# Two-layer graph network: four leaky activations, a maximum and a propagator moved to the far side of the copies of zT

## The chip, the cores and the metric

The kernel runs on one core of a Trainium2 chip. The metric is the device time of one execution in microseconds. Before the change the median of three runs is 2470.5 us (2469.41 to 2471.38). The profiled execution spans 2467.1 us.

The engines are named as in the profile: PE (matrix products; PEld is its loading of weights), DVE (vector), ACT (scalar, activations and copies out of PSUM), POOL (GpSimd) and SP, which only issues DMAs here. Each engine works through its own list of instructions in order. An instruction that waits for another engine holds up everything behind it on its own engine.

## The reference

The input is 128 graphs of 128 nodes with 512 features, `x`, and 128 adjacency matrices of zeros and ones, `adj`. Two layers follow each other, each with a residual and a layer norm:

```python
# layer 0: graph attention, 8 heads of 64
feats = einsum('bnf,hfu->bhnu', x, W)
dense = e_self[..., :, None] + e_neigh[..., None, :]
dense = leaky_relu(dense, 0.2) + NEG_BIG * (1 - A)
att = softmax(dense, axis=-1)
x = layernorm(x + relu(einsum('bhij,bhju->bhiu', att, feats) + b))

# layer 1: two hypergraph convolutions, 512 -> 1024 -> 512
def hypergraph_conv(x, adj, W, b):      # H = (adj != 0)
    xw = einsum('ncd,hd->nch', x, W)
    m = Be * einsum('nce,nch->neh', H, xw)
    return Dn * einsum('nce,neh->nch', H, m) + b
h = layer_norm(relu(hypergraph_conv(x, adj, W1, b1)), gamma, beta)
x = layernorm(x + hypergraph_conv(h, adj, W2, b2) + x)
```

`Dn` and `Be` are reciprocal degrees of nodes and hyperedges. The kernel folds the two products with `H` and both degrees into one 128x128 matrix for each graph, the propagator `R`.

## The kernel before

The graphs are taken in 64 pairs. The work on one pair is cut into some hundred steps, small functions such as `propagate` or `leaky`. Each step has a lag in whole periods and a due time within a period of `T = 38.6`; the step of pair `p` is due at `(p + lag) * T + time`. All steps of all pairs are sorted by due time, and every engine gets its instructions in that order. The due times are only an order: nothing is timed by them. A dictionary `first` gives some steps of the first pairs a due time of their own. A tile framework adds the semaphore waits: an instruction waits for the data it reads, and an instruction that writes a tile waits until the readers of the tile that had the same memory before are done. Tiles come from pools; `work` has one buffer a tag unless `bufs` says otherwise, and PSUM is a ring of eight banks under the tag `bank`.

In the steady state four stages of different pairs lie beside each other in one period. The part around the change, for the pair that is in its second layer ("this pair") and the one a period behind ("the next pair"):

- `first_output` (L780, ACT): writes the normalised result of layer 0 into `y`, for both graphs of this pair.
- `propagate` (L802, PE): `y` times `R`, eight instructions a graph in the trace, into the banks `pz`. `z_evict` (L813, ACT) copies each bank to `zT`. `z_sums` (L822, POOL) makes four sums `zS` from it.
- `hidden` in `chain("ph", 3, ...)` (L833, L846, PE): seven products with the first hidden weights. They use a Strassen-like scheme with seven instead of eight block products. Four of the seven go into the same bank, `phX`. Their order is product 1 (into phX), 2 (phY), 6 (phX), 5 (phW) and 7 (phX), then the two products `pq` of an older pair, then 4 (phX) and 3 (phW). Between two uses of `phX` ACT copies the bank out (`copy`, L329, with `nc.scalar.copy` at L332) and PE then adds the next product on top.
- `masked`, `leaky`, `largest`, `exponential` (L576 to L609): attention of the next pair, for each graph `g` and half of the heads `q`. POOL adds the mask, ACT applies the leaky activation in four instructions (L595), DVE takes the maximum (L601), ACT takes four exponentials (L609). All work in place in the tile `nb`. Then SP writes the result out and reads it back in blocks (L613, L621), and DVE transposes it (L630).
- `propagator` and `r_evict` (L427, L437): two 128x128 products `pd` from `hB` and `hT` (PE, four instructions), and DVE's scaling of it to `R`. `R` is first read one period later. It has three buffers.
- `edges` (L400, DVE): for the pair after the next one. It transposes blocks of the adjacency into `hT` (L409), counts (L411), and makes reciprocal degrees `deg` (L415, L416). `hT` has one buffer, so the write of `hT` for one pair comes after the propagator's reading of `hT` for the pair before.
- `sum_rest` (L960, DVE): sums of squares for the norm of `h`, which came back through DRAM (`so`, `veh`). POOL turns them into `rsh` (L986), DVE scales `y2` by it (L994), and `output` (L1004, PE, `pq`) reads the scaled `y2`.

Before the change the order on PE is: the last `py` products of this pair's predecessor with `pd` between them, then `pz`, then the first `phX`. On ACT it is: `first_output`, eight leaky activations (graph 0), a copy to `y2` (L922), the two copies to `zT`, four leaky activations, the first copy of `phX`, eight exponentials, four leaky activations, the second copy of `phX`, eight exponentials, the third copy. On DVE: `hT`, `deg`, `R`, two maxima, a sum of `y2` (L924), `so` and `veh`, a maximum, a sum of `h` (L855), the scaling of `y2`, a maximum.

Of the kernel before, what the change touches and what calls it, by code (L numbers as in the profile page):

```python
# [20 lines left out]
def kernel(  # L21
# [67 lines left out]
    def bank(name):  # L89
        return psum.tile([P, HALF], F32, tag="bank", name=name)  # L90
# [210 lines left out]
    LAST = PAIRS - 1  # L301
    steps = []

    def step(lag, time, since=0, until=PAIRS):

        def keep(fn):
            steps.append((lag, time, fn.__name__, range(since, until), fn, ()))
            return fn
        return keep

    def at(lag, time, fn, *args, since=0, until=PAIRS):
        steps.append((lag, time, fn.__name__, range(since, until), fn, args))
# [111 lines left out]
                s["hB"][:, g, :], s["hT"][:, g, :], s["be"][:, g:g + 1], None, op0=ALU.mult  # L424
            )

    @step(1, 34.7)  # L427
    def propagator(p, s):

        s["pd"] = bank(f"pd_{p}")  # L430
        for g in range(2):
            nc.tensor.matmul(
                s["pd"][:, g * N:(g + 1) * N], s["hB"][:, g, :], s["hT"][:, g, :],
                start=True, stop=True,
            )

    @step(1, 35.8)  # L437
    def r_evict(p, s):
        s["R"] = work.tile([P, 2, N], F32, tag="R", name=f"R_{p}", bufs=3)
        nc.vector.tensor_tensor(  # L440
            s["R"].rearrange("p g (b n) -> p g b n", b=NB),
            s["pd"][:, :2 * N].rearrange("p (g b n) -> p g b n", g=2, b=NB),
            s["dnb"].rearrange("p b g n -> p g b n"), op=ALU.mult,
        )
# [199 lines left out]
        )  # L644

    for (g, q), tm, (lag, tl), (lagx, tx), te, tt in (
        ((0, 0), 31.0, (1, 33.2), (1, 36.1), 4.05, 16.6), ((0, 1), 32.2, (1, 35.0), (1, 36.7), 4.6, 16.65),
        ((1, 0), 34.2, (2, 2.05), (2, 2.1), 7.8, 21.5), ((1, 1), 35.4, (2, 6.0), (2, 7.3), 7.9, 21.55),
    ):
        at(1, tm, masked, g, q)  # L650
        at(lag, tl, leaky, g, q)
        at(lagx, tx, largest, g, q)
        at(2, te, exponential, g, q)
        at(2, tt, e_transpose, g, q, since=1)
# [254 lines left out]
    def weigh(s, i, to, start):  # L909
# [3 lines left out]
          QU, 1, until=LAST)  # L913
# [43 lines left out]
                s["sd"][:, 2 * c:2 * c + 2, :].rearrange("b g n -> b (g n)"),  # L957
            )

    @step(4, 1.0, until=LAST - 1)  # L960
    def sum_rest(p, s):
        t = work.tile([P, B], F32, tag="so", name=f"so_{p}")
        nc.vector.transpose(t, sums_out)
        s["ve"] = small.tile([P, 2], F32, tag="ve", name=f"veh_{p}")
        nc.vector.tensor_reduce(
            s["ve"], t[:, :2 * NB].rearrange("p (b g) -> p g b", g=2), AX.X, ALU.add
        )
# [147 lines left out]
    for t, fn, *args in (  # L1115
# [44 lines left out]
        ("spread_rows", 1): 15.72, ("nodes", 1): 15.55, ("write_nodes", 1): 15.85,  # L1160
        ("edges", 1): 110.4, ("scale_edges", 1): 110.5, ("neighbours", 1): 80.1,
        ("propagator", 1): 117.76, ("spread_nodes", 1): 80.3, ("r_evict", 1): 121.8,
        ("leaky", 0, 1, 1): 77.65,
        ("attend", 0, 0, 0): 78.95, ("attend", 0, 0, 1): 78.96, ("attend", 0): 97.85,
        ("attended", 0, 0): 99.7, ("attended", 0, 1): 99.8,
        ("leaky", 1, 0, 0): 117.85, ("leaky", 1, 0, 1): 117.9, ("leaky", 1, 1, 0): 119.9,
        ("largest", 1, 0, 0): 118.0, ("largest", 1, 0, 1): 118.2, ("largest", 1, 1, 0): 120.2,
        ("masked", 1, 0, 0): 109.0, ("masked", 1, 1, 1): 121.5,
        ("nodes", 2): 141.0, ("write_nodes", 2): 143.0, ("nodes", 3): 150.0,
        ("write_nodes", 3): 150.1, ("skip", 0): 132.5,  # L1170
    }

# [88 lines left out]
```

## Time and profile before

| | PE | PEld | DVE | ACT | POOL |
|---|---|---|---|---|---|
| busy, us of 2467.1 | 2411.5 | 2148.6 | 1997.5 | 1529.3 | 1797.7 |
| share of the span | 98% | 87% | 81% | 62% | 73% |
| instructions | 18273 | 18273 | 4456 | 4481 | 2060 |

The granted PE clock is 9 tenths or more in each of the 40 slices of the page, and the DMA engines are busy for 0.4 to 0.6 of each but the last two. PE's busy time counts a matmul from its start to its modelled end, and neighbouring matmuls overlap, so a busy PE isn't a PE at its peak. What can be read is where PE is idle: an idle time stands in square brackets after an instruction, with what ended it. A timeline line is: start, length, engine, line, operation, output<-inputs, shapes, how many instructions were merged.

Some costs from the groups of the page and of the trace: a product of `pd`, `pz` or `ph` has a mean of 275 to 281 ns from start to modelled end; a leaky activation 391 ns, an exponential 392 ns, a copy of `phX` 580 ns, all from start to end, with starts closer together than that when they follow each other; a maximum 682 ns; the scaling to `R` 409 ns.

### The profile page before, as it was taken

The page shows a single profiled execution, that of the slowest core. Times are in us where ns is not written, and L with a number is a line of the kernel's source. Part 1 is how long each engine was busy: PE and PEld are TensorE (multiplying, and loading weights), DVE is VectorE, ACT ScalarE, POOL GpSimd, SP SyncE. Part 2 cuts the span into 40 slices and gives each one's busy share as a digit, 9 for nine tenths or more (in the row PEclk, how much of TensorE's full clock was granted, in tenths as well). Part 3 has the DMA queues.
Part 4 walks back from the last instruction along what each step waited for, and adds up shares of the span by engine and source line. Part 5 has one row for each costly group of instructions (what it writes and reads, how often), then busy time and mean ns, then how long its engine had stood idle before and what let it go on. Part 6 is the DMA issues. An engine that isn't in the chain of part 4 may idle for free.

```text
span 2467.1 us, 52770 instructions
## 1 busy us (share of the span) xinstructions
PE 2411.5 (98%) x18273; PEld 2148.6 (87%) x18273; DVE 1997.5 (81%) x4456; ACT 1529.3 (62%) x4481; POOL 1797.7 (73%) x2060
## 2 busy tenths in 40 slices
PE   7999999999999999999999999999999999999998
PEld 5888888888888888888888888888888888888887
DVE  7888788888878887888788888878887888788876
ACT  4565665755756656657566566576575665665763
POOL 5777777777777777767777777777677767777774
PEclk9999999999999999999999999999999999999999
DMA  6545445545445455454455555554544545545531
GB/s 183 137 145 144 145 130 148 146 129 151 141 137 146 143 145 145 128 153 138 134 145 145 142 142 141 148 145 129 151 138 136 147 139 146 143 135 153 142 112 52
DMA packets 432762, 345.30 MB, mean 140 GB/s; under 512 B 153176, under 2 KB 382064, under 8 KB 432496
## 3 DMA queue, kind: packets, MB, share of 16 engines
q1 hardware_dynamic: 429024, 337.46, 48.3%
q10 hardware_dynamic: 3472, 4.47, 0.5%
q8 instruction: 145, 2.38, 0.4%
q14 instruction: 121, 0.99, 0.1%
HBM read 239.08 MB, written 102.73 MB: 139 GB/s over the span
## 4 chain that ended last, share of the span: by engine, by line
PE 55%; DVE 14%; ACT 11%; DMA 11%; POOL 5%; issue 4%; SPq 2%; DVEq 0%; POOLq 0%; ACTq 0%
PE phX L840 17%; PE phW L840 8%; PE pfX L476 8%; ACT nb L595 6%; PE pyX L476 4%; PE phY L840 4%; PE pfW L476 4%; DMA sd<-sr 4%; PE pq L1006 4%; DMA nb<-rd 3%; DVE y L725 3%; ACT y L782 2%; DVE xT L373 2%; DVE y L739 2%; PE pfY L476 2%
## 5 line engine op out<-in xcount | busy, mean ns | idle before, releaser
L332 ACT COPY py<-pyX 128x257 f32<-128x257 f32 x189 | 70.9, 375 | 531.1 <-PE pyX L476 526.6
L840 PEld LDWEIGHTS phX<-zS,w_sb 128*128 128x128 f32 x3072 | 363.1, 192 | 33.0 <-issue 31.6
L840 PE MATMUL phX<-zS,w_sb 128*128 128x128 f32 x3072 | 374.3, 275 | 2.4 <-POOL xS L458 1.3
L893 POOL TENSOR_TENSOR sq<-sq 128x512 f32<-128x512 f32 (+2 forms) x384 | 324.0, 844 | 20.4 <-ACT sq L881 0.3
L579 POOL TENSOR_TENSOR nb<-nb,neg 128x512 f32<-128x512 f32 x256 | 318.5, 1277 | 9.2 <-DMA nb<-rd 9.2
L595 ACT ACTIVATE nb<-nb,ft 128x128 f32<-128x128 f32 x1020 | 317.9, 391 | 7.9 <-POOL nb L579 7.9
L755 POOL TENSOR_TENSOR rso<-veo,mhalf 128x2 f32<-128x2 f32 x63 | 44.2, 701 | 371.6 <-DVE veo L753 371.6
L609 ACT ACTIVATE nb<-nb,nm 128x128 f32<-128x128 f32 x1024 | 313.6, 392 | 0.6 <-DVE nm L601 0.6
L870 ACT ACTIVATE h<-h,vecs 128x128 f32<-128x128 f32 x768 | 244.9, 392 | 42.3 <-DVE h L855 42.3
L476 PE MATMUL pyX<-w_sb,hS 128*128 128x257 f32 x1008 | 245.6, 385 | 0.0
L476 PE MATMUL pyW<-w_sb,hS 128*128 128x256 f32 x1008 | 238.7, 379 | 3.1 <-DVE y L924 2.9
L476 PE MATMUL pyX<-w_sb,h 128*128 128x257 f32 x1008 | 239.5, 379 | 0.5 <-ACT py L332 0.5
L601 DVE TENSOR_REDUCE nm<-nb 128x4 f32<-128x512 f32 x256 | 174.5, 682 | 73.0 <-ACT nb L595 60.7
L476 PEld LDWEIGHTS pyW<-w_sb,hS 128*128 128x128 f32 x1008 | 190.5, 189 | 31.4 <-POOL rsa L755 3.2
L476 PEld LDWEIGHTS pyX<-w_sb,hS 128*128 128x128 f32 x1008 | 185.8, 189 | 28.7
L476 PEld LDWEIGHTS pyX<-w_sb,h 128*128 128x128 f32 x1008 | 186.5, 190 | 25.5 <-ACT py L332 0.9
L499 DVE TENSOR_TENSOR ft<-pf,pfW 128x264 f32<-128x264 f32 x124 | 53.2, 429 | 165.8 <-PE pfW L476 90.1
L630 DVE STREAM_TRANSPOSE eT<-eb 128x512 f32<-128x512 f32 x252 | 163.5, 687 | 0.0
L881 ACT ACTIVATE sq<-h 128x512 f32<-128x512 f32 x256 | 160.4, 627 | 2.1
L730 POOL TENSOR_TENSOR y<-y,b_bc 128x512 f32<-128x512 f32 x128 | 160.3, 1273 | 1.8 <-DVE rden L724 1.5
L458 POOL TENSOR_TENSOR hS<-h 128x512 f32<-128x512 f32 x126 | 158.9, 1281 | 2.3 <-ACT h L870 2.3
L840 PE MATMUL phX<-zT,w_sb 128*128 128x128 f32 x1024 | 131.1, 281 | 26.1 <-ACT zT L817 26.1
(178 smaller groups left out, 5783.5 us busy)
## 6 DMA issues: line engine op xcount, KB each, us to landing
nb<-rd SPq DMA_DIRECT2D x127, 512.0 KB
ed<-nb SPq DMA_DIRECT2D x126, 512.0 KB
eb<-ed SPq DMA_DIRECT2D x504, 128.0 KB
x<-in_x_dram SPq DMA_DIRECT2D x64, 512.0 KB
out_dram<-o SPq DMA_DIRECT2D x63, 512.0 KB
xb<-in_x_dram SPq DMA_DIRECT2D x248, 128.0 KB
a<-in_adj_dram SPq DMA_DIRECT2D x64, 128.0 KB
w<-in_adj_dram SPq DMA_DIRECT2D x128, 64.0 KB
```

Source lines behind the costliest of these rows:

```text
L458: engine.tensor_tensor(t[:, i], in0, in1, op=op)
L476: nc.tensor.matmul(to[:, :n], lhs[:, k, :], rhs[:, k, :n], start=bool(start) and k == 0, stop=(k == nk - 1), skip_group_check=True,)
L579: nc.gpsimd.tensor_tensor(t, t, neg[:, :, None, :].to_broadcast([P, NB, HH, B]), op=ALU.add)
L595: nc.scalar.activation(t, t, AF.Prelu, bias=s["ft"][:, g, h, 0:1], alpha=SLOPE)
L601: nc.vector.tensor_reduce(s["nm"][:, g, hs], scores(p, s, g, hs).rearrange("p b h j -> p h b j"), AX.XY, ALU.max, negate=True,)
L609: nc.scalar.activation(t, t, AF.Exp, bias=s["nm"][:, g, h:h + 1])
L630: nc.vector.transpose(s["eT"][:, g, hs, :].rearrange("p h (b i) -> p h b i", b=NB), s["eb", g][:, :, hs, :].rearrange("p b h j -> p h b j"),)
L730: nc.gpsimd.tensor_tensor(s["y"][:, g, :], s["y"][:, g, :], b0_bc, op=ALU.add)
L840: nc.tensor.matmul(to[:, m * N:(m + 1) * N], w[:, k, m * P:(m + 1) * P], rhs[:, k, :], start=bool(start) and m == 0 and k == 0, stop=(k == ...
L870: nc.scalar.activation(dst[:, k, :], src[:, k, :], AF.Relu, bias=b1_sb[:, c:c + 1])
L881: nc.scalar.activation(s["sq"][:, g, q * KH // 2:(q + 1) * KH // 2, :], hid(s, g, q), AF.Square, scale=DH ** -0.5,)
L893: nc.gpsimd.tensor_tensor(t[:, :n, :], t[:, :n, :], t[:, n:2 * n, :], op=ALU.add)
```

## The change

Three moves, all by due times alone; no instruction is added or removed.

1. On ACT and DVE, the leaky activations of graph 0, second half of the heads (four instructions), and their maximum move behind the two copies of `zT`, to lag 1 at 40.63 and 40.68, which is 2.03 and 2.08 into the period of the propagation.
2. On PE, the next pair's propagator moves from between the last `py` products to between `propagate` and the first hidden product (40.1 is 1.5 into that period). DVE's `r_evict` follows it, and `sum_rest` goes behind that.
3. In the prologue, pair 1 has no step of the first kind to move around, so the old due times of its second half are kept (73.6 and 75.3), and `nodes` of pair 2 is due a step later.

The aim is that ACT comes to the copies of `zT` sooner, and that PE has the propagator's products to do while the copy is made.

```diff
-    @step(1, 34.7)
+    @step(1, 40.1)
     def propagator(p, s):
...
-    @step(1, 35.8)
+    @step(1, 40.2)
     def r_evict(p, s):
...
     for (g, q), tm, (lag, tl), (lagx, tx), te, tt in (
-        ((0, 0), 31.0, (1, 33.2), (1, 36.1), 4.05, 16.6), ((0, 1), 32.2, (1, 35.0), (1, 36.7), 4.6, 16.65),
+        ((0, 0), 31.0, (1, 33.2), (1, 36.1), 4.05, 16.6), ((0, 1), 32.2, (1, 40.63), (1, 40.68), 4.6, 16.65),
         ((1, 0), 34.2, (2, 2.05), (2, 2.1), 7.8, 21.5), ((1, 1), 35.4, (2, 6.0), (2, 7.3), 7.9, 21.55),
...
-    @step(4, 1.0, until=LAST - 1)
+    @step(4, 1.7, until=LAST - 1)
     def sum_rest(p, s):
...
-        ("leaky", 0, 1, 1): 77.65,
+        ("leaky", 0, 1, 1): 77.65, ("leaky", 0, 0, 1): 73.6, ("largest", 0, 0, 1): 75.3,
...
-        ("nodes", 2): 141.0, ("write_nodes", 2): 143.0, ("nodes", 3): 150.0,
+        ("nodes", 2): 142.2, ("write_nodes", 2): 143.0, ("nodes", 3): 150.0,
```

## The prediction

> **What bounds the kernel now.** I read the page's busy shares first: PE is busy for 2411.5 us of 2467.1 (98%), so time can come only from PE's few gaps. Second, the busy sums over two windows, each one pair long (the start of one propagation to the start of the next): both last 37.7 us, PE is idle for 0.4 of it, and no other engine passes 31 us. Third, the table of waits says what that 0.4 us is.
>
> ```profile
> 1037.46:1075.17 37.71, 37.28 (x285) 33.33 (x284) 30.90 (x70) 23.84 (x71) 27.91 (x33) 1.00 0.50 143
> 1075.17:1112.90 37.73, 37.33 (x286) 33.37 (x285) 30.92 (x71) 23.86 (x72) 27.93 (x33) 1.00 0.48 142
> ```
> (Columns: length, busy us of PE, PEld, DVE, ACT, POOL, clock, DMA share, GB/s.)
>
> ```profile
> PEld phX L840 <- ACT zT L817: 37.7, 61, 0.9
> PE phX L840 <- ACT zT L817: 26.1, 61, 0.7
> ```
> 61 times, once a pair, the first hidden product waits for ACT's copy of zT. Last, the timeline around one such wait; all instants below are of this window:
>
> ```profile
> 1071.27 0.61 PE L432 MATMUL pd<-hT,hB 128*128 128x128 f32 x4
> 1071.71 1.90 PE L476 MATMUL pyX<-w_sb,h 128*128 128x256 f32 x8
> ...
> 1072.44 4.98 POOL L579 TENSOR_TENSOR nb<-nb,neg 128x512 f32<-128x512 f32 x4
> ...
> 1072.89 1.50 ACT L782 ACTIVATE y<-y,sh,rsa 128x512 f32<-128x512 f32 x2
> 1072.92 0.44 DVE L409 STREAM_TRANSPOSE hT<-ab 128x256 f32<-128x256 f32 x1
> ...
> 1073.93 1.04 DVE L415 TENSOR_SCALAR deg<-deg 128x2 f32<-128x2 f32 x1
> 1074.30 2.43 ACT L595 ACTIVATE nb<-nb,ft 128x128 f32<-128x128 f32 x8
> ...
> 1075.17 1.95 PE L805 MATMUL pz<-R,y 128*128 128x128 f32 x16
> ...
> 1076.89 1.06 ACT L817 COPY zT<-pz 128x512 f32<-128x512 f32 x2
> ...
> 1077.52 2.05 PE L840 MATMUL phX<-zT,w_sb 128*128 128x128 f32 x16 [0.40 <-ACT zT L817]
> ...
> 1079.41 1.95 PE L840 MATMUL phY<-zT,w_sb 128*128 128x128 f32 x16
> ...
> 1079.61 0.59 ACT L332 COPY ph<-phX 128x512 f32<-128x512 f32 x1 [0.48 <-PE phX L840]
> 1080.09 2.45 ACT L609 ACTIVATE nb<-nb,nm 128x128 f32<-128x128 f32 x8
> ...
> 1083.61 0.56 ACT L332 COPY ph<-phX 128x512 f32<-128x512 f32 x1
> ...
> 1084.77 1.95 PE L840 MATMUL phX<-zS,w_sb 128*128 128x128 f32 x16
> ```
> ACT runs eight leaky activations (0.293 us apart) and a copy before the copies of zT; PE has finished the propagation long before. The real price is more than 0.40: with no wait, 16 matmuls follow in 1.79 us (phY 1079.41 to the next product 1081.20), so from pz at 1075.17 phY would start at 1078.74. It starts at 1079.41: **0.67 us a pair**, made of 0.16 of drain, 0.40 of idle and 0.11 at the first matmul after the wait.
>
> **What the Trainium skill says.** "GPSIMD Engine Reference", Specifications: GpSimd's SBUF interfaces are shared with VectorE, with contention for DVE instructions in a 2-port mode or with two SBUF inputs. "Advanced Engine Details and Errata", Instruction Support: tensor_scalar has such a mode, tensor_reduce none. The trace agrees: deg, a tensor_scalar on 128x2, takes 169 ns at least and 1056 ns in the median; above, it ends at 1074.97, just after the second of POOL's four masks of 1.28 us; the reductions L601 keep to 682 ns beside the same masks. "DVE: scalar operands, raw-bit mode, write accounting and state across instructions", Flops that outlive an instruction, calls the DVE's queue one in-order queue; in this trace the DVE never overtakes a waiting instruction.
>
> **The change, part by part.**
>
> *Propagator behind the propagation (PE).* Nothing is added: 4 matmuls of 0.111 us apiece, 0.44 us, leave their place at 1071.27 and come after pz. So pz starts at 1074.73. Its input is ready: the two activations L782 start 0.70 us apart and take 0.80, so y is there at 1073.69 and 1074.39. pd runs from 1076.51, and the first hidden product can follow at 1076.95, phY at 1078.74, the third and fourth products at 1080.52 and 1082.31, the fifth (third use of phX) at 1084.10 where it was 1084.77. The gap is filled: **-0.67**.
>
> *Four leaky activations behind the copies (ACT).* Four leave, 1.17 us. ACT reaches zT at 1075.72 and waits for PE: first half of pz done at 1075.78, so the copy runs 1075.82 to 1076.40, in time for 1076.95; the second runs 1076.71 to 1077.29. Then eight activations (2.35) and the copy of phX at 1079.55, where it was 1079.61. ACT thus stays where it was, while PE goes 0.67 earlier. Each copy of phX must end before PE adds the next product into that bank. First copy: ends 1080.14, needed 1080.52, no wait. Second: from the first copy to the second it is 4.00 us now (8 exponentials, 4 leaky, a copy), so 1083.55 to 1084.11, plus 0.05 of signalling (zT ends 1077.47, PE starts 1077.52), against 1084.10: a wait of 0.06, and again 0.11 at the first matmul: **+0.17**. Third: behind pq, over half a microsecond to spare.
>
> *A new wait on the DVE.* hT has one buffer. The next pair's edges write it (L409, 1072.92) after the old propagator has read it; in the program as built, that transposition now waits for the moved pd. pd drains at 1076.95 + 0.16 = 1077.12, so hT starts at 1077.16, 4.24 us later, and everything queued behind it on the DVE waits too: deg, the first maximum, a sum of y2, R, the sums of squares, the second maximum, and with it four exponentials on ACT and its next copy of phX. What it costs hangs on deg. hT to deg is 1.01 us: deg at 1078.17. POOL then makes zS: first 1077.38 to 1078.11 (0.73), second from 1078.19 (starts are 0.81 apart before). So deg meets a hole of 0.08 us, takes 0.17, and the first maximum starts at about 1078.47 (0.13 after deg, by recip and R before). From it to the second maximum: 0.61 + 0.30 + 0.31 + 0.25 + 0.09 = 1.56 (starts of maximum, y2, R, so, veh), so 1080.03, done 1080.71. The exponentials ask for the first maximum at 1080.03 (done 1079.15) and for the second at 1081.20. **0**, with 0.5 to spare. If deg misses the hole it ends with the second zS, at 1078.95: second maximum 1081.32, exponentials 0.16 late.
>
> *The reduction of sums a step later, R and a maximum later (DVE).* 0: R is next read a pair later; the sums' transposition waited for a DMA before (39.2 us in total, 34 times) and now comes after it. pq asks for its y2 at about 1086, y2's scaling ends near 1084.2.
>
> *Banks, prologue.* The ring of eight banks shifts by one place between pd and pfX; each bank's last reader is microseconds earlier: 0. The three changed due times of the prologue touch single instructions: 0, ±2 us.
>
> Sum: -0.67 + 0.17 = -0.50 a pair, 61 times: -30.5, so **2440 us**.
>
> **Rivals.**
> - A, as above: 2440. For it: the hole, and deg's 169 ns in the few pairs where the mask ended as it came. Against it: the margin is 0.02 us.
> - B, deg misses the hole: copy 0.16 later, wait 0.22 + 0.11, net -0.34, -21: 2450.
> - C, deg takes its 1.04 us as now: ends 1079.21, second maximum 1081.58, exponentials 0.42 late, wait 0.48 + 0.11, net -0.08: 2466, no change. The lengths tied to POOL speak against it.
> - D, deg gets in only behind the third zS (1079.60): both maxima late, exponentials 0.84 late, wait 0.90 + 0.11, net +0.34: 2491, slower. deg passes between two masks that follow without a hole, which speaks against it.
> - E, no wait on the second copy and no 0.11: the whole -0.67, 2430.
>
> **Numbers.** A 0.40, B 0.27, E 0.13, C 0.11, D 0.09. Unknown small shifts of 0.1 us in the DVE chain are 6 us. The range 2427 to 2461 holds E, A and B with that margin and leaves out C and D. Faster 0.79 (E, A, B less a little), same 0.10 (C), slower 0.11 (D and what I don't see).
>
> **What would show it.** In the profile after: pairs 37.2 us long; no wait of phX for zT; DVE idle 4 us before hT, released by PE pd; deg near 0.2 us (A) or 0.75 (B); PE phX waiting for ACT ph some 0.1 us a pair. A wait of ACT's exponentials for a maximum above 0.4 us, or of PE for y or y2, would make it wrong.

## The result, and the profile after

| | before | after |
|---|---|---|
| time, us (median, lowest to highest of 4 runs each) | 2470.9 (2469.4 to 2471.4) | 2450.3 (2450.1 to 2450.9) |
| ratio to before, 95% interval | | 0.9918 [0.9901, 0.9935] |
| one pair, us (the two windows of each trace) | 37.71, 37.73 | 37.40, 37.40 |
| DVE busy, us | 1997.5 | 1906.3 |

The change takes 20.5 us off, 0.8%. The forecast was 2440, 30.5 us less than before.

The page after: its busy times, and the shares of the chain of work that ended last.

```profile
PE 2419.9 (99%) x18273; PEld 2146.3 (88%) x18273; DVE 1906.3 (78%) x4456; ACT 1528.1 (62%) x4481; POOL 1803.8 (74%) x2060
...
PE 96%; DVE 2%; DMA 1%; ACT 1%; issue 0%; POOL 0%; SPq 0%; POOLq 0%; DVEq 0%; ACTq 0%
```

PE's share of the chain rises from 55% to 96%. That looks as if nothing but PE were left, and it is nearly so; the rest of this text is about the 0.36 us a pair that this line hides. The busy sums of a window after, from one propagation to the next:

```profile
1030.16:1067.56 37.40, 37.40 (x286) 33.27 (x285) 29.32 (x69) 23.83 (x72) 28.03 (x34) 1.00 0.53 149
```

PE is busy for the whole pair. Yet the pair is 0.18 us longer than the 37.22 that the forecast's working gives, so some products take longer than their pitch while they count as busy. The table of waits after:

```profile
DVE hT L409 <- PE pd L432: 264.2, 61, 4.4
...
PEld pyW L476 <- issue: 17.7, 61, 0.5
```

The two waits of `phX` for the copy of `zT` are gone. DVE now stands before `hT` for 264.2 us, 61 times, released by `pd`: the new wait of the forecast. And one line is new that the forecast didn't have: before the loading of weights for `pyW`, 61 times, once a pair. It is booked as "issue", which names no releaser. In the kernel before this line read 0.9 us in 2 times. (`pyX` and `pyW` are banks of the products with the second hidden weights, a chain like that of `ph`; L924 on DVE sums such banks into `y2`.) The timeline after, from the last `py` products to the third use of `phX`:

```profile
1063.96 1.89 PE L476 MATMUL pyX<-w_sb,h 128*128 128x256 f32 x8
...
1065.22 0.38 DVE L924 TENSOR_TENSOR y<-py,pyW 128x256 f32<-128x256 f32 x1
...
1065.72 1.60 PEld L476 LDWEIGHTS pyW<-w_sb,hS 128*128 128x128 f32 x8 [0.27 <-issue]
1065.75 1.97 PE L476 MATMUL pyW<-w_sb,hS 128*128 128x256 f32 x8
...
1067.56 1.95 PE L805 MATMUL pz<-R,y 128*128 128x128 f32 x16
...
1069.34 0.61 PE L432 MATMUL pd<-hT,hB 128*128 128x128 f32 x4
...
1069.79 1.95 PE L840 MATMUL phX<-zT,w_sb 128*128 128x128 f32 x16
...
1069.99 0.45 DVE L409 STREAM_TRANSPOSE hT<-ab 128x256 f32<-128x256 f32 x1 [4.38 <-PE pd L432]
...
1071.00 0.17 DVE L415 TENSOR_SCALAR deg<-deg 128x2 f32<-128x2 f32 x1
1071.01 0.74 POOL L828 TENSOR_TENSOR zS<-zT,zS 128x256 f32<-128x256 f32 x1
...
1071.57 1.95 PE L840 MATMUL phY<-zT,w_sb 128*128 128x128 f32 x16
...
1075.15 1.95 PE L840 MATMUL phW<-zS,w_sb 128*128 128x128 f32 x16
...
1076.36 0.56 ACT L332 COPY ph<-phX 128x512 f32<-128x512 f32 x1
...
1077.07 2.02 PE L840 MATMUL phX<-zS,w_sb 128*128 128x128 f32 x16
...
1078.93 1.46 PE L1006 MATMUL pq<-y,R 128*128 128x512 f32 x3
```

The same sum and the same product in the kernel before:

```profile
1072.63 0.38 DVE L924 TENSOR_TENSOR y<-py,pyW 128x256 f32<-128x256 f32 x1
...
1073.44 1.89 PE L476 MATMUL pyW<-w_sb,hS 128*128 128x256 f32 x8
```

Since PE shows no idle time in these lines of after, read it by the distance between starts. Without a wait, eight instructions with 128x256 results follow in 1.73 us (before: `pyX` 1071.71, `pyW` 1073.44, `pz` 1075.17) and sixteen with 128x128 results in 1.79. These distances are called the bare pitch below.

- `pz` to the first `phX`: 2.23 us, with `pd`'s 0.44 inside. The rest, 1.79, is the bare pitch: the gap is filled.
- `pyX` to `pyW`: 1.79, and `pyW` to `pz`: 1.81, against 1.73 each. Over all pairs that is 0.074 and 0.077 us, 0.15 together. The last `pyW` product adds into the bank that DVE's sum of `y2` (L924) has just read; that ends at 1065.60, and the weights load starts at 1065.72. Before, the same sum ended at 1073.01, 0.43 ahead of PE.
- `phW` to the third use of `phX`: 1.92, and from there to `pq` (1078.93): 1.86, against 1.79 each. Over all pairs 0.138 and 0.072, 0.21 together. ACT's copy ends at 1076.92, within 0.02 us of the moment at which PE would have been there (1076.94).

Together that is the 0.36.

### The profile page after: what moved, and what is told of

The parts are those of the page before. It is cut to its first block, busy times and chain, and to the rows that moved or that the text cites. A ratio compares the mean times of both kernels' runs of the same rounds, so it can differ in the third digit from the quotient of the medians.

```text
span 2448.5 us, 52709 instructions
## 1 busy us (share of the span) xinstructions
PE 2419.9 (99%) x18273; PEld 2146.3 (88%) x18273; DVE 1906.3 (78%) x4456; ACT 1528.1 (62%) x4481; POOL 1803.8 (74%) x2060
## 4 chain that ended last, share of the span: by engine, by line
PE 96%; DVE 2%; DMA 1%; ACT 1%; issue 0%; POOL 0%; SPq 0%; POOLq 0%; DVEq 0%; ACTq 0%
PE phX L840 19%; PE pyX L476 18%; PE pyW L476 9%; PE phW L840 9%; PE pfX L476 9%; PE pav L693 5%; PE pz L805 5%; PE phY L840 5%; PE pfW L476 4%; PE pq L1006 4%; PE pyY L476 4%; PE pfY L476 2%; PE pd L432 1%; PE pf L513 1%; PE py L1052 0%
## 5 line engine op out<-in xcount | busy, mean ns | idle before, releaser
L893 POOL TENSOR_TENSOR sq<-sq 128x512 f32<-128x512 f32 (+2 forms) x384 | 329.6, 858 | 20.3 <-ACT sq L881 0.3
L476 PE MATMUL pyW<-w_sb,hS 128*128 128x256 f32 x1008 | 243.9, 384 | 2.5 <-DVE y L924 2.2
L409 DVE STREAM_TRANSPOSE hT<-ab 128x256 f32<-128x256 f32 x62 | 27.6, 445 | 264.2 <-PE pd L432 264.2
L601 DVE TENSOR_REDUCE nm<-nb 128x4 f32<-128x512 f32 x256 | 169.2, 681 | 7.0 <-ACT nb L595 6.0
L730 POOL TENSOR_TENSOR y<-y,b_bc 128x512 f32<-128x512 f32 x128 | 160.1, 1272 | 1.9 <-DVE y L704 1.5
```

The source lines that it names most:

```text
L476: nc.tensor.matmul(to[:, :n], lhs[:, k, :], rhs[:, k, :n], start=bool(start) and k == 0, stop=(k == nk - 1), skip_group_check=True,)
L601: nc.vector.tensor_reduce(s["nm"][:, g, hs], scores(p, s, g, hs).rearrange("p b h j -> p h b j"), AX.XY, ALU.max, negate=True,)
L730: nc.gpsimd.tensor_tensor(s["y"][:, g, :], s["y"][:, g, :], b0_bc, op=ALU.add)
L893: nc.gpsimd.tensor_tensor(t[:, :n, :], t[:, :n, :], t[:, n:2 * n, :], op=ALU.add)
```

## The experiments

Each ratio is to runs of the kernel before on the same chip (medians 2471.5 for experiments 1, 2, 4 and 5, 2470.3 for the others). "After" below is the changed kernel; edits are to it where nothing else is said. The expectations call experiment 2 e2 and experiment 4 e3.

**1. The stall of DVE before `hT`.** A second buffer for `hT` takes the wait away; a constant used only in the set-up moves into a work buffer to make room.

```diff
-        hT = work.tile([P, 2, N], F32, tag="hT", name=f"hT_{p}")
+        hT = work.tile([P, 2, N], F32, tag="hT", name=f"hT_{p}", bufs=2)
...
+    as_bc = work.tile([P, F], F32, tag="y", name="as_bc")
```

> The changed kernel with two buffers for hT, so that the DVE's transposition no longer waits for the propagator (as_bc moves into the memory of y, which is not used yet, to make room). Theory: the 4.4 us in which the DVE stands before hT lie beside other work, so the pair keeps 37.40 us and the time stays at 2450, within 3 us; deg goes back to about 1 us beside the masks, and the wait of hT for pd is gone. Rival: the stall is what keeps the change from its forecast of 37.22 us a pair; then the pair falls to about 37.2 and the time to about 2440.

Measured: 2451.9 us (2450.5 to 2452.5), ratio 0.992 [0.9906, 0.9933], no better than after. No wait of `hT` for `pd` is left in its trace, `deg` goes back to a median of 1052 ns, and the wait at `pyW` stays as it was (17.1 us in 59 times). The distances between PE's products stay as well, at the third `phX` too (1.92). So 264 us of DVE standing still cost nothing.

**2. The sum of `y2` sooner.** On DVE a transposition of the next input (`xT`, L373, 1.10 us) stands just before L924. Here it goes behind.

```diff
-    at(0, 30.85, x_transpose, 1, since=2)
+    at(0, 34.5, x_transpose, 1, since=2)
```

> The changed kernel with the second transposition of x (1.1 us of DVE) due behind the sum of y2 that frees the bank pyW (34.5 for 30.85). Theory: the last pyW product, which is 0.44 us earlier without the propagator ahead of it, now waits for that sum on the DVE (PE loses 0.15 us a pair, booked as issue); with the sum 1.1 us earlier the loss is gone: 37.25 us a pair, 2450 - 9 = 2441. Rival: the 0.15 us is PE's own issue (its weights or its queue), which the DVE's order doesn't touch: 2450.

Measured: 2441.2 us (2440.3 to 2441.6), ratio 0.9877 [0.9863, 0.989]. Its timeline around the last `py` products and the third `phX`:

```profile
1059.12 1.89 PE L476 MATMUL pyX<-w_sb,h 128*128 128x256 f32 x8
1060.86 1.89 PE L476 MATMUL pyW<-w_sb,hS 128*128 128x256 f32 x8
1062.59 1.95 PE L805 MATMUL pz<-R,y 128*128 128x128 f32 x16
...
1070.17 1.95 PE L840 MATMUL phW<-zS,w_sb 128*128 128x128 f32 x16
1072.10 2.02 PE L840 MATMUL phX<-zS,w_sb 128*128 128x128 f32 x16
```

Both distances at `pyW` are 1.73 to 1.74 again, and the line of waits for it is gone; the loss at the third `phX` is still there (1.93). The pair is 37.25 us, 0.15 less than after. The line booked as "issue" was a wait for DVE, and it cost 9 us.

**3. The same edit in the kernel before.** If the earlier `xT` were a loss of its own, whatever the change, it would show here.

> Control: the kernel before with the second transposition of x behind the sum of y2, the edit of e2. Theory: before, the propagator's 0.44 us ahead of the last two y products keeps PE behind the DVE's sum, so the wait for it doesn't exist and there is nothing to gain: 2470, within 3 us. Rival: the order of the DVE is worth 9 us by itself, and e2 says nothing of the change: 2461.

Measured: 2468.5 us (2467.3 to 2469.9), ratio 0.9995 [0.9987, 1.0004]; a pair 37.70. It brings nothing there that is clear of the noise, where experiment 2 brought 9 us, so the wait at `pyW` came with the change.

**4. The second copy of `phX` sooner.** The second leaky activations of graph 1, which ACT does before that copy, go behind it.

```diff
-        ((1, 0), 34.2, (2, 2.05), (2, 2.1), 7.8, 21.5), ((1, 1), 35.4, (2, 6.0), (2, 7.3), 7.9, 21.55),
+        ((1, 0), 34.2, (2, 2.05), (2, 2.1), 7.8, 21.5), ((1, 1), 35.4, (2, 7.6), (2, 7.62), 7.9, 21.55),
```

> The changed kernel with the last four leaky activations and their maximum behind the second copy of phX (7.6 and 7.62 for 6.0 and 7.3). Theory: the third product into phX waits for that copy (0.14 us before it and 0.07 at its first matmul, 0.21 a pair); the copy comes 1.0 us earlier and the loss is gone: 37.19 us a pair, 2450 - 13 = 2437. Rival: the time comes back behind it, because the maximum of these activations and all that follows on the DVE are 0.4 us later, and the sum of h that frees phW with them: 2445 to 2455.

Measured: 2450.2 us (2449.5 to 2451.5), ratio 0.9915 [0.9902, 0.9929]: the expected gain isn't there. The timeline says where it went:

```profile
1063.96 1.89 PE L476 MATMUL pyX<-w_sb,h 128*128 128x256 f32 x8
1065.97 1.97 PE L476 MATMUL pyW<-w_sb,hS 128*128 128x256 f32 x8
...
1075.37 1.95 PE L840 MATMUL phW<-zS,w_sb 128*128 128x128 f32 x16
1077.15 1.95 PE L840 MATMUL phX<-zS,w_sb 128*128 128x128 f32 x16
```

The third `phX` follows at the bare pitch, 1.78. But `pyX` to `pyW` is now 2.01 instead of 1.79: the 0.21 us came back whole at the next wait. L924 starts 32.84 us after the first `phX` here and in after alike (medians over the pairs). It doesn't follow PE between these two places, and a PE that comes sooner only waits longer for it. The time lies in the range of the expectation's rival, but the way isn't the rival's: `phW` shows no wait, the next one is that of `pyW`.

**5. Both edits (2 and 4).**

> Both edits of e2 and e3. If the two losses are separate, they add: 37.40 - 0.15 - 0.21 = 37.04 us a pair, 2450 - 22 = 2428, and PE has no wait left in the steady state. If one hides behind the other, 2437.

Measured: 2430.6 us (2429.4 to 2430.9), ratio 0.9834 [0.982, 0.9847], a pair 37.07. With L924 out of the way, edit 4 is worth 10.6 us. This is the best version: 19.7 us under after, 40.9 under before. It lies 0.03 us a pair over the expectation. That stands at one `pfX` product: from it to the next are 0.917 us, where experiment 2 has 0.890 (means), and the loading of its weights has a new wait for POOL (`rso`, 9.8 us in 54 times). In this kernel `deg` takes 448 ns in the median: it comes while POOL's first sum of `zS` still runs, and no loss of PE shows for it.

**6. The leaky activations and the maximum alone** (edit to the kernel before, with their two entries for pair 1; the propagator stays where it was).

```diff
-        ((0, 0), 31.0, (1, 33.2), (1, 36.1), 4.05, 16.6), ((0, 1), 32.2, (1, 35.0), (1, 36.7), 4.6, 16.65),
+        ((0, 0), 31.0, (1, 33.2), (1, 36.1), 4.05, 16.6), ((0, 1), 32.2, (1, 40.63), (1, 40.68), 4.6, 16.65),
```

> The kernel before with the leaky activations and their maximum moved alone (propagator, R and the reduction of sums where they were). Theory: zT is copied in time and the 0.67 us at the first phX goes, but ACT doesn't come earlier to the copies of phX, while PE does: waits of 0.24 at the second and 0.41 at the third product into phX take its place. Sum -0.03 a pair, 2464 to 2470. Rival: the leaky move is the change, and the propagator only a filler: 2440 to 2450.

Measured: 2470.7 us (2467.7 to 2471.6), ratio 1.0 [0.9992, 1.0009]. Its timeline:

```profile
1074.50 1.95 PE L805 MATMUL pz<-R,y 128*128 128x128 f32 x16
1076.28 2.00 PE L840 MATMUL phX<-zT,w_sb 128*128 128x128 f32 x16
1078.12 1.95 PE L840 MATMUL phY<-zT,w_sb 128*128 128x128 f32 x16
1080.03 2.02 PE L840 MATMUL phX<-zS,w_sb 128*128 128x128 f32 x16
1081.89 1.95 PE L840 MATMUL phW<-zS,w_sb 128*128 128x128 f32 x16
1084.02 1.24 PE L840 MATMUL phX<-zS,w_sb 128*128 128x128 f32 x9 [0.17 <-ACT ph L332]
```

The first `phX` follows `pz` after 1.78: the wait for `zT` is gone. In its place the next distances are 1.84, 1.91, 1.86 and 2.13, so 0.58 over four pitches of 1.79, and 0.07 more behind the last: 0.65, where 0.67 was won. ACT makes the copies of `phX` no sooner than before, and PE now waits for those.

**7. The propagator alone** (edit to the kernel before: the due times of `propagator`, `r_evict` and `sum_rest`, and `nodes` of pair 2).

```diff
-    @step(1, 34.7)
+    @step(1, 40.1)
     def propagator(p, s):
```

> The kernel before with the propagator (and R, the reduction of sums, and the prologue's step) moved alone; the eight leaky activations stay ahead of the copies of zT. Theory: ACT reaches zT no earlier, so the first phX starts where it did; the propagator only fills the wait that its leaving makes longer: 2468 to 2473, with a wait of phX for zT still there once a pair. Rival: the propagator's 0.44 us is hidden in the gap whatever ACT does: 2444.

Measured: 2490.1 us (2488.7 to 2491.0), ratio 1.008 [1.0067, 1.0094]: slower by some 20 us, where 2468 to 2473 was expected. Its timeline:

```profile
1043.28 1.89 PE L476 MATMUL pyX<-w_sb,h 128*128 128x256 f32 x8
1045.51 1.97 PE L476 MATMUL pyW<-w_sb,hS 128*128 128x256 f32 x8 [0.33 <-DVE y L924]
1047.31 1.95 PE L805 MATMUL pz<-R,y 128*128 128x128 f32 x16
1049.09 0.61 PE L432 MATMUL pd<-hT,hB 128*128 128x128 f32 x4
1049.89 2.05 PE L840 MATMUL phX<-zT,w_sb 128*128 128x128 f32 x16 [0.19 <-ACT zT L817]
```

`pyX` to `pyW` to `pz` is 2.23 and 1.80, 0.57 over two bare pitches: here the wait names its releaser, L924. And `pz` to `phX` is still 0.35 over, with 0.11 behind it, since ACT's four leaky activations stand before the copy. 1.03 lost where the kernel before loses 0.67; the pair is 38.08. L924 comes 0.3 us later after the first `phX` here than in after (33.16 against 32.84). The waits show the way there:

```profile
POOL veh L989 <- DVE veh L965: 19.5, 61, 0.7
DVE y L996 <- POOL rsh L992: 12.7, 60, 1.4
```

In after these two come 1 time each. Here two maxima stand ahead of DVE's `so` and `veh`, where after has one, so `veh` comes 0.47 later after the first `phX` (medians over 40 pairs), POOL waits for it, and DVE waits for `rsh` before it scales `y2`. DVE catches up later, where it stands and waits for PE, but POOL carries the delay on: the second of its two bias additions (L730) is still 0.33 late, and DVE's L739, which runs beside it and ahead of L924, ends 0.54 after it in both kernels. This is read from the traces; no run takes the delay away.

The parts alone give 0 and +20 us, together -20. Each needs the other.

**8. The hole that `deg` meets.** On top of the edit of experiment 2, one more small DVE instruction ahead of `deg`, so that it comes too late for the gap between two sums of `zS`. Its result isn't used.

```diff
+        if p >= 2:
+            nc.vector.reciprocal(small.tile([P, 2], F32, tag="spare", name=f"spare_{p}"), deg)
```

> e2 with one more instruction on the DVE, a reciprocal of 128x2 into a spare tile (0.17 us, 0.2 with its wait), ahead of deg. Theory: deg now comes at POOL's second zS instead of into the hole before it, and waits for its end: about 0.6 us instead of 0.17; with the reciprocal the second maximum is 0.62 later, 0.24 more than it has to spare, and ACT's copy and PE follow: 2441 + 15 = 2456. Rival: deg isn't held, the 0.2 us fit into the 0.38 to spare: 2441.

Measured: 2459.9 us (2458.0 to 2460.4), ratio 0.9957 [0.9944, 0.9969]; a pair 37.57 against 37.25. The summary of `deg` with the edit of experiment 2 alone, and in this kernel, where L415 has become L417 (count, then shortest, median and longest ns):

```profile
L415 DVE TENSOR_SCALAR deg<-deg x64: 168/170/737, 21.3 to 2332.7; 128x2 f32<-128x2 f32 x64
...
L417 DVE TENSOR_SCALAR deg<-deg x64: 169/712/748, 23.1 to 2352.4; 128x2 f32<-128x2 f32 x64
```

Two waits of this kernel:

```profile
PE phX L842 <- ACT ph L332: 19.0, 57, 0.8
...
ACT nb L611 <- DVE nm L603: 13.9, 54, 0.6
```

An instruction of 0.17 us makes `deg` 0.54 longer: in one pair `deg` starts at 1074.72, 0.04 after POOL's second sum of `zS`, and ends at 1075.43, 0.02 after it. The maxima come later, the exponentials with them, and PE waits at the third `phX`. The second copy of `phX` ends 0.35 later than with the edit of experiment 2 alone (7.49 against 7.14 after the first `phX`, medians). The pair is 0.32 longer, some 19 us in all for one instruction a pair. Case B's mechanism is real; it was absent from after by 0.01 us, the time by which `deg` starts before that sum there.

## Why the prediction was right, and where its size failed

- **Propagator behind the propagation, -0.67.** The gap itself is filled as forecast: `pz` to the first `phX` is 0.12 shorter than before although `pd`'s 0.44 lie inside it now, and `phX` to `phY` is 0.11 shorter, so 0.67. What failed is the step "Its input is ready". That looked at `y` for `pz`, but `pd` had stood ahead of two more products, the last `pyX` and `pyW`. They too come 0.44 us sooner, and the last `pyW` waits for L924. Before, L924 ended 0.43 us ahead of that product. After, it ends 0.09 ahead of the bare pitch (1065.69), and PE's start follows 0.15 behind it. The mis-sized term is +0.15 a pair, which the forecast put at 0 by not looking at it, measured by experiment 2 (9.1 us) with experiment 3 as its counterpart.
- **Second copy of `phX`, +0.17.** Mechanism right, size 0.21. The copy ended where it was forecast (9.38 us after `pz` by the working, 9.36 in the trace). The mis-sized term is the signalling: 0.05 was taken from the copy of `zT`, a wait for data, and here, where the product waits for its bank, it starts 0.15 after the copy's end. The first matmul behind it costs 0.07, not 0.11. Experiment 5 against 2 gives 10.6 us for this wait.
- **New wait on the DVE, 0.** Right: 4.38 us long against 4.24 forecast, 61 times, and experiment 1 shows that it costs nothing. The first maximum, whose input ACT has ready at 1068.17, stands behind it until 1071.31.
- **`deg` in the hole.** Right, in every pair, by less than forecast: `deg` starts at 1071.00 and the second sum of `zS` at 1071.01. Its 64 instructions take 10.8 us together, a mean of 169 ns, where they took 61.8 and 965 before; 51 of the 91 us that DVE is busy less are this one instruction. They don't shorten the kernel: experiment 1 has a median of 1052 ns again, early in the pair where there is time, at nearly the same speed.
- **Banks, the move of the sums.** Nothing in the trace speaks against 0. The prologue's ±2 us were not measured apart.

The sum by these terms: -0.67 + 0.21 + 0.15 = -0.31 a pair, 61 times -19; measured -20.5. The time is that of case B (2450), but its cause isn't: `deg` did not miss the hole, and the 10 us that A lacks are the wait at `pyW`, with 0.04 a pair more at the third `phX`. The range reached so far for the sake of B, so it is by luck that it holds 2450 for another reason. Experiment 5, with both waits gone, comes to 2430.6, the figure of rival E. The forecast's own list of what would make it wrong (a wait of PE "for y or y2") fits the wait at `pyW`; in the profile it appears under "issue", without that name.

## What to carry to other kernels

When an instruction is moved behind others, everything between its old and its new place comes sooner: go through each of those instructions and compare the end of what it waits for, not only the one that the move was made for. Here a gap on the bounding engine was won only as far as the later waits within the period had slack: experiments 4 and 6 removed a wait and got nothing, and experiment 4's edit was worth 10.6 us once the next wait was out of the way. With PE always busy in the profile, take distances between starts against the bare pitch of the same products, and look at "issue" before a weight load when its count is once a period.

## What the hardware showed that was not expected

A producer that is only just on time still costs PE 0.15 to 0.2 us in after: PE's product starts 0.15 us after the end of what it waited for (copy 1076.92, product 1077.07; L924 1065.60, product 1065.75), and the distance to the next product is 0.07 to 0.08 longer. Both are waits for a bank; behind the copy of `zT`, before, it was 0.05 and 0.11. Why the two differ isn't shown. "GPSIMD Engine Reference" of the Trainium skill, Specifications, says that VectorE and GpSimd share SBUF interfaces; that agrees with a `deg` that ends with POOL's sum. How much hangs on the moment is the surprise: `deg` takes 170 ns in experiment 2 and 712 ns in experiment 8 (medians), where one instruction of 0.17 us stands ahead of it.
